# Where the last batch is cut: 24 of its 32 feed-forward steps over all 512 tokens, eight over halves, with the down projection of those eight summed on token partitions

## The chip, the core and the metric

The kernel runs on one core of a Trainium2 chip. The metric is the device time of one execution in microseconds (us). Matrix products run on the tensor engine (PE; its weight loads are shown as a row of their own, PEld), element-wise work on VectorE (DVE), ScalarE (ACT) and GpSimd (POOL). SyncE (SP) issues most of the transfers between on-chip memory and DRAM.

## What is computed

Eight batches of 512 tokens with 128 channels, all float32. For each batch, an attention part with linear cost, and then a dense sum over eight experts:

```python
x = x + layernorm(attention(layernorm(x)))
z = layernorm(x)
acc = 0
for wg, wu, wd in zip(Wg, Wu, Wd):          # 8 experts, 128 -> 512 -> 128
    acc += (silu(z @ wg) * (z @ wu)) @ wd
x = x + layernorm(acc)
```

The expert sum holds nearly all of the arithmetic: 8 experts times 4 slices of 128 hidden features are 32 steps for each batch.

## The kernel before

Channels (or hidden features) lie on the partitions and tokens along the free axis during a step. A step `i` takes one slice of 128 features: two products `g` (L928) and `u` (L930) with the weights `wg`, `wu` as the stationary operand and the normed tokens `zT` as the moving one; ACT makes `sg = silu(g)` (L932), and DVE makes `h = sg * u` (L939). The down projection then sums `wd.T @ h` over all 32 steps in PSUM. The order of instructions on each engine is the order in which the program issues them; no scheduler moves them. `g` and `u` have two PSUM buffers each, so the `u` product of step i+2 needs the `h` of step i to be done.

The work is cut into `units`. Batches 1 to 6 are one unit each, `WHOLE`, with 512 tokens. Batches 0 and 7 are two units each, `HALVES`, with 256 tokens and 32 steps.

- In a half unit, `down` (L768) is issued `LAG` = 2 steps after its `h`: one 128x256 product a step into `accA`, channels on the partitions.
- In a whole unit, the down projection goes over pairs of steps with seven block products in place of eight (Strassen's scheme). POOL makes the combinations `t` of `h` (L953 to L955), and `down_pairs` (L783, matmuls at L823) works off eight pairs at a time (`GROUP` = 16 steps), at step 17 of its unit and at step 1 of the next one, into the two banks `accA` and `accB`.
- `Last` finishes a whole batch during the next unit: `turn` (called at steps 2 and 3) transposes one bank in 32x32 blocks on DVE (`f_blkA`, `f_blkB`, L602) and `carry` (L261) sends it through DRAM by one write (L264) and four reads (L266) on SP's queue, which completes the transposition into `fA` and `fB`. Later `add` (seven DVE operations, L616 to L623) puts the seven products together into `q`, `stats`, `scales` and `norm` do the layer norm, and SP stores the result.
- The accumulator of a half unit has the same bank `accA`, of which there is one buffer.
- A half unit's sum is finished by a copy (L777), PE transposes (L258) and a norm in `finish`; the very last one by `finish_last` (L701): a copy by DVE and one by ACT (L717), two PE transposes (L721), bn_stats (L724), aggregation (L726), the power on POOL (L728), scaling, adding the residual and two stores (L737).

`plan(n)` names the step at which each of these pieces is issued, and `between(n)` runs them: at each step after `h` and before the down projections that have come due.

Of the kernel before, what the change touches and what calls it, by code (L numbers as in the profile page):

```python
# [16 lines left out]
def kernel(  # L17
# [10 lines left out]
    wd: bass.AP,  # L28
    out: bass.AP,
):  # L30

# [25 lines left out]
    nc = tc.nc  # L59
# [200 lines left out]

    def carry(dst, blocks):  # L261

        t = dram.tile([P, NQ, P], F32, tag="bounce", name="bounce")
        nc.sync.dma_start(t, blocks)  # L264
        for q in range(NQ):
            nc.sync.dma_start(  # L266
                dst[q * Q : (q + 1) * Q], t[:, q, :].rearrange("(r i) c -> i r c", r=NQ)
            )
# [21 lines left out]
        return t.rearrange("p j c -> p (j c)")  # L290

    def parts(b):
        return HALVES if b in (0, B - 1) else WHOLE

    x2s, zTs, rest = {}, {}, []

# [295 lines left out]
    class Last:  # L592
# [3 lines left out]
        def __init__(self, b, sums):  # L596
            self.b, self.sums, self.f = b, sums, []

        def turn(self):
            name = "AB"[len(self.f)]  # L600
            t = work.tile([P, NQ, P], F32, tag=f"blk{name}", name=f"f_blk{name}_{self.b}")
            nc.vector.transpose(  # L602
                t.rearrange("p a (s j k) -> p a s j k", s=2, j=2),
                self.sums[len(self.f)].rearrange("c (s a j i) -> c a s j i", s=2, a=NQ, j=2),
            )
            self.f.append(work.tile([P, NQ, P], F32, tag=f"f{name}", name=f"f{name}_{self.b}"))
            carry(self.f[-1], t)

        def add(self):
            A, D = (t.rearrange("p (t b) (s x) -> p t s b x", t=2, s=2) for t in self.f)  # L610
# [87 lines left out]
        nc.gpsimd.tensor_tensor(o, o, flat(x2s[b][:, r]), ALU.add)  # L698
        nc.sync.dma_start(out[b].rearrange("(p j) c -> p j c", j=NJ)[:, r], fn[:, :n])

    def finish_last(b, lo, hi, acc):  # L701


        n = hi - lo
        stats = small.tile([P, n, 6], F32, tag=f"stats{n}", name="stats_last")
        mv = small.tile([P, n, 2], F32, tag=f"mv{n}", name="mv_last")
        rstd = small.tile([P, n], F32, tag=f"rstd{n}", name="rstd_last")
        ve = small.tile([P, n], F32, tag=f"ve{n}", name="ve_last")
        fT = work.tile([P, N], F32, tag="fT", name="fT_last")
        fn = work.tile([P, NJ, C], F32, tag="fn", name="fn_last")  # L710
        o = work.tile([P, NJ, C], F32, tag="x1", name="o_last")
        acc = acc.rearrange("c (a j i) -> c a j i", a=NQ, j=n)
        dst = out[b].rearrange("(p j) c -> p j c", j=NJ)
        f_ps = []
        for j in range(n):
            cols = slice(j * P, (j + 1) * P)
            (nc.scalar.copy if j else nc.vector.tensor_copy)(  # L717
                fT[:, cols].rearrange("c (a i) -> c a i", a=NQ), acc[:, :, j]
            )
            t = ps.tile([P, N], F32, tag="ps", name=f"f_ps_last{j}")  # L720
            nc.tensor.transpose(t[:, :P], fT[:, cols], ident)  # L721
            f_ps.append(t)
        for j in range(n):
            nc.vector.bn_stats(stats[:, j, :], f_ps[j][:, :C])  # L724
        for j in range(n):
            nc.vector.bn_aggr(mv[:, j, :], stats[:, j, :])  # L726
        nc.vector.tensor_scalar_add(ve, mv[:, :, 1], EPS)
        nc.gpsimd.tensor_tensor(rstd, ve, mhalf[:, :n], ALU.pow)  # L728
        for j in range(n):
            nc.vector.tensor_scalar(  # L730
                fn[:, j, :], f_ps[j][:, :C], mv[:, j, 0:1], rstd[:, j : j + 1],
                ALU.subtract, ALU.mult,
            )
            (nc.vector if j else nc.gpsimd).tensor_tensor(
                o[:, j, :], fn[:, j, :], x2s[b][:, lo + j], ALU.add
            )
            (nc.scalar if j else nc.sync).dma_start(dst[:, lo + j], o[:, j, :])  # L737

    units = [(b, lo, hi) for b in range(B) for lo, hi in parts(b)]
    NSTEP = E * NF  # L740
    LAG = 2
    GROUP = 16
    HALF = C // 2
    accs, fins = {}, {}
    due = []
# [14 lines left out]
                    yield  # L760

    def down(n, i, h):
        b, lo, hi = units[n]
        if i == 0:
            accs[n] = ps_acc.tile([P, N], F32, tag="accA", name=f"acc_{n}")
        e, f = divmod(i, NF)
        cols = (hi - lo) * P
        nc.tensor.matmul(  # L768
            accs[n][:, :cols], wd_sb[e][:, f, :], h, start=(i == 0), stop=(i == NSTEP - 1)
        )  # L770
        if i == NSTEP - 1:
            acc = accs.pop(n)[:, :cols]
            if n == len(units) - 1:
                finish_last(b, lo, hi, acc)
                return
            fT = work.tile([P, N], F32, tag="fT", name=f"fT_{n}")
            nc.vector.tensor_copy(  # L777
                by_block(fT[:, :cols], hi - lo),
                acc.rearrange("c (a j i) -> c a j i", a=NQ, j=hi - lo),
            )  # L780
            fins[n] = finish(b, lo, hi, fT[:, :cols])

    def down_pairs(n, g, pairs):  # L783

        b, lo, hi = units[n]
        if g == 0:
            accs[n] = [  # L790
                ps_acc.tile([P, N], F32, tag=f"acc{t}", name=f"acc{t}_{n}") for t in "AB"
            ]
        A, D = accs[n]
        low, high = slice(0, HALF), slice(HALF, C)
        left, right = slice(0, N // 2), slice(N // 2, N)
        last = NSTEP // 2 - 1
        for two in range(0, len(pairs), 2):
            below, above = [], []
            for m, (h, t) in enumerate(pairs[two : two + 2]):
                k = g * GROUP // 2 + two + m  # L800
                e, pair = divmod(k, NF // 2)
                w0, w1 = wd_sb[e][:, 2 * pair], wd_sb[e][:, 2 * pair + 1]
                sm = ws_sb[e][:, pair]


                first, end = k == 0, k == last
                below += [
                    (A[low, left], w0[:, low], h[:, 0], first, False),
                    (A[low, right], w1[:, low], h[:, 2], False, end),
                    (D[low, right], sm[:, 3], h[:, 3], first, end),  # L810
                ]
                above += [
                    (D[high, right], sm[:, 0], t[:, 0], first, False),
                    (A[high, right], sm[:, 1], t[:, 2], first, False),
                    (D[high, left], sm[:, 2], t[:, 1], False, end),
                ]
                if m == 0:
                    below.append((D[low, left], w1[:, high], t[:, 3], False, False))
                else:
                    above.append((A[high, left], w1[:, high], t[:, 3], False, end))  # L820
            for two_tiles in zip(below, above):
                for o, w, r, start, stop in two_tiles:
                    nc.tensor.matmul(o, w, r, start=start, stop=stop)  # L823
        if (g + 1) * GROUP == NSTEP:
            fins[n] = Last(b, accs.pop(n))

    attentions = {}
# [5 lines left out]
    def plan(n):  # L833

        b, lo, hi = units[n]
        p = {i: [] for i in range(NSTEP)}

        def at(i, *calls):  # L840
            p[i] += calls

        following = attentions[b + 1] if 0 < b < B - 1 else None
        second = opened(b + 2) if hi == NJ and b + 2 < B else None
# [21 lines left out]
        if hi < NJ or lo:  # L866
            if second:
# [2 lines left out]
                at(23, second.norm)  # L870
                at(24, second.turn)
                at(31, second.affine)
            if last:
                at(14, last("add"))
                at(16, last("stats"))
                at(18, last("scales"))
                at(21, last("norm"))
        else:
            if second:
                at(17, second.stats, second.scales)  # L880
# [10 lines left out]

    def between(n):

        b, lo, hi = units[n]
        if lo == 0 and b + 2 < B:
            xs[b + 2] = load_x(b + 2)
        going = rest[:]
# [4 lines left out]
        if n == 1:  # L902
            going.append(attention(1))
        p = plan(n)
        for i in range(NSTEP):
            if isinstance(fins.get(n - 1), type(weight_sums())):
                going.append(fins.pop(n - 1))
            going = [g for g in going if next(g, "end") != "end"]
            for call in p[i]:
                call()  # L910
            yield
# [1 line left out]

    opening()
    count = 0
    for n, (b, lo, hi) in enumerate(units):
        zT = zTs.pop((b, lo))
        whole = hi - lo == NJ
        cols = (hi - lo) * P
        if whole:  # L920
            zT = zT.rearrange("c a (h j) i -> c h a (j i)", h=2)
            pairs = []
        others = between(n)
        for i in range(NSTEP):
            e, f = divmod(i, NF)
            w = bass.ts(f, P)
            g_ps = ps_gu.tile([P, N], F32, tag="g", name=f"g_{n}_{i}")
# [8 lines left out]
                h = flat(h2[:, 2 * (i % 2) : 2 * (i % 2) + 2])  # L936
            else:
                h = hp.tile([P, N // 2], F32, tag="h", name=f"h_{n}_{i}")
            nc.vector.tensor_tensor(h, sg[:, :cols], u_ps[:, :cols], ALU.mult)  # L939
            if not whole:  # L940
                due.append((count + LAG, partial(down, n, i, h)))
            elif i % 2:
                t2 = pairp.tile([P, 4, N // 2], F32, tag="t2", name=f"t2_{n}_{i}")
                pairs.append((h2, t2))
                if len(pairs) == GROUP // 2:
                    due.append((count + LAG, partial(down_pairs, n, i // GROUP, pairs)))
                    pairs = []
            next(others)
# [7 lines left out]
            count += 1  # L956
        for _ in others:
            pass
    for _, call in due:
        call()  # L960


# [29 lines left out]
```

## Time and profile before

| | |
|---|---|
| median of 3 runs | 708.70 us (708.69 to 709.01) |
| the profiled execution | 709.01 us |
| its span in the profile | 707.1 us |
| mean granted PE clock | 0.995 |
| PE busy | 692.7 us, 98% |
| POOL busy | 352.7 us, 50% |
| DVE busy | 299.0 us, 42% |
| ACT busy | 247.8 us, 35% |

A share is busy time over the span. Matmuls are pipelined, and the profile models their ends, so the busy time of PE overstates how full it is; for its pace the distance between the starts of successive matmuls is read. A float32 product of 128x128 by 128xN shows as two weight loads and two matmul records. The rows of a timeline give the start, the duration, the engine, the line, the operation, output and inputs, their sizes, how many instructions were merged, and in brackets how long the engine had been idle and what released it. The chain of waits merges neighbours in time, so its rows give a start and a length.

The last batch begins at 603.65 us, where its first `g` starts, and the span ends at 707.1 us.

### The profile page before, as it was taken

What the parts mean: (1) busy time and instruction counts of PE and PEld (TensorE: products, weight loads), DVE (VectorE), ACT (ScalarE), POOL (GpSimd) and SP (SyncE); (2) the same over time, 40 slices, a digit from 0 to 9 for tenths busy, and PEclk for the clock granted to TensorE, in tenths of its full rate; (3) what the DMA queues carried; (4) which work ended last, traced back from release to release, by engine and by line L of the source; (5) the groups of instructions that cost most, each with busy time, mean ns of one, the idle gap of its engine ahead of it and who ended that gap; (6) DMA issues with size and microseconds to landing.
All of it is one profiled execution on the core that took longest, in us unless ns stands there. A gap on an engine that the chain in (4) does not pass through costs nothing.

```text
span 707.1 us, 9148 instructions
## 1 busy us (share of the span) xinstructions
PE 692.7 (98%) x3149; PEld 420.2 (59%) x3149; DVE 299.0 (42%) x832; ACT 247.8 (35%) x497; POOL 352.7 (50%) x445
## 2 busy tenths in 40 slices
PE   8998999999999999999999999999999999999996
PEld 5787886454454545545455554555445454688885
DVE  5534463553425533354415634256332534134433
ACT  3322435334424334243333434334351423123231
POOL 3721121875647767385745867377673757301000
PEclk9999999999999999999999999999999999999998
DMA  8400001002011200102001020111101010010000
GB/s 265 156 1 0 8 0 58 25 1 75 0 53 37 71 21 29 60 1 90 0 31 59 17 75 0 45 45 47 31 15 64 12 46 1 1 59 17 8 0 8
DMA packets 31774, 27.14 MB, mean 38 GB/s; under 512 B 3440, under 2 KB 24176, under 8 KB 31728
## 3 DMA queue, kind: packets, MB, share of 16 engines
q1 hardware_dynamic: 31440, 26.36, 11.5%
q8 instruction: 25, 0.41, 0.3%
q14 instruction: 21, 0.17, 0.1%
q10 hardware_dynamic: 288, 0.20, 0.1%
HBM read 16.58 MB, written 9.96 MB: 38 GB/s over the span
## 4 chain that ended last, share of the span: by engine, by line
PE 93%; DVE 2%; issue 2%; POOL 1%; ACT 1%; DMA 0%; DVEq 0%; POOLq 0%
PE g L928 31%; PE u L930 30%; PE accA L823 12%; PE accB L823 9%; PE acc L768 7%; PE y_ps L559 1%; PE g_ps L476 1%; PE k_ps L534 1%; POOL rstd L186 0%; DMA x<-in_L_attn_x_dram 0%; DVE stats L180 0%; PE z_ps L258 0%; POOL x L450 0%; DVE stats L196 0%; POOL rstd L208 0%
## 5 line engine op out<-in xcount | busy, mean ns | idle before, releaser
L939 DVE TENSOR_TENSOR h<-sg,u 128x512 f32<-128x512 f32 (+1 forms) x320 | 185.5, 581 | 373.5 <-PE u L930 356.9
L932 ACT ACTIVATE sg<-g 128x512 f32<-128x512 f32 (+1 forms) x320 | 163.4, 512 | 397.9 <-PE g L928 375.1
L928 PE MATMUL g<-zT,wg 128*128 128x512 f32 (+1 forms) x640 | 274.4, 510 | 0.9 <-DVE zT L684 0.7
L930 PE MATMUL u<-zT,wu 128*128 128x512 f32 (+1 forms) x640 | 272.9, 508 | 0.2 <-DVE h L939 0.2
L930 PEld LDWEIGHTS u<-zT,wu 128*128 128x128 f32 x640 | 121.5, 190 | 99.7 <-issue 89.7
L953 POOL TENSOR_TENSOR t<-h 128x512 f32<-128x512 f32 x96 | 121.9, 1270 | 117.6 <-DVE h L939 117.6
L928 PEld LDWEIGHTS g<-zT,wg 128*128 128x128 f32 x640 | 118.1, 191 | 83.6 <-issue 74.9
L823 PE MATMUL accB<-t,ws 128*64 128x256 f32 x384 | 107.0, 381 | 0.0
L823 PE MATMUL accA<-h,wd 128*64 128x256 f32 x384 | 99.2, 381 | 0.0
L768 PE MATMUL acc<-h,wd 128*128 128x256 f32 x256 | 76.4, 381 | 1.3 <-DVE f_blkA L602 1.3
L954 POOL TENSOR_TENSOR t<-h,t 128x256 f32<-128x256 f32 x96 | 69.7, 726 | 7.5
L955 POOL TENSOR_TENSOR t<-h,t 128x256 f32<-128x256 f32 x96 | 69.6, 725 | 7.5
L823 PEld LDWEIGHTS accA<-h,wd 128*64 128x64 f32 x384 | 51.6, 137 | 34.7 <-issue 4.9
L823 PE MATMUL accA<-t,ws 128*64 128x256 f32 x192 | 57.1, 379 | 0.0
L823 PE MATMUL accB<-h,ws 128*64 128x256 f32 x192 | 57.1, 379 | 0.0
L234 POOL TENSOR_TENSOR rstd<-ve,mhalf 128x4 f32<-128x4 f32 (+1 forms) x24 | 28.1, 1170 | 54.1 <-DVE nm L232 46.7
L768 PEld LDWEIGHTS acc<-h,wd 128*128 128x128 f32 x256 | 47.9, 191 | 9.0 <-issue 3.1
L823 PEld LDWEIGHTS accB<-t,ws 128*64 128x64 f32 x384 | 51.6, 137 | 0.0
L823 PEld LDWEIGHTS accB<-h,ws 128*64 128x64 f32 x192 | 26.3, 137 | 13.9
L823 PE MATMUL accB<-t,wd 128*64 128x256 f32 x96 | 28.6, 379 | 0.0
L823 PE MATMUL accA<-t,wd 128*64 128x256 f32 x96 | 28.6, 379 | 0.0
L823 PEld LDWEIGHTS accA<-t,ws 128*64 128x64 f32 x192 | 26.3, 137 | 0.0
(185 smaller groups left out, 407.1 us busy)
## 6 DMA issues: line engine op xcount, KB each, us to landing
wg<-in_L_ffn_Wg_dram SPq DMA_DIRECT2D x8, 256.0 KB, 6.0
wu<-in_L_ffn_Wu_dram SPq DMA_DIRECT2D x8, 256.0 KB, 5.9
wd<-in_L_ffn_Wd_dram SPq DMA_DIRECT2D x8, 256.0 KB, 6.1
x<-in_L_attn_x_dram SPq DMA_DIRECT2D x7, 256.0 KB, 3.0
bounce<-xh_blk SPq DMA_DIRECT2D x6, 256.0 KB, 2.1
xhT<-bounce SPq DMA_DIRECT2D x24, 64.0 KB, 2.0
bounce<-ek_blk SPq DMA_DIRECT2D x6, 256.0 KB, 2.0
ek<-bounce SPq DMA_DIRECT2D x24, 64.0 KB, 2.0
```

The source lines that it names most:

```text
L234: nc.gpsimd.tensor_tensor(rstd, ve, mhalf[:, :n], ALU.pow)
L476: nc.tensor.matmul(g_ps[:, :C], xh[:, j, :], ek[:, :, j * Q : (j + 1) * Q], start=(j == 0), stop=(j == NJ - 1),)
L534: nc.tensor.matmul(k_ps, w_qkv_sb[:, C : 2 * C], self.xnT, start=True, stop=True)
L768: nc.tensor.matmul(accs[n][:, :cols], wd_sb[e][:, f, :], h, start=(i == 0), stop=(i == NSTEP - 1))
L823: nc.tensor.matmul(o, w, r, start=start, stop=stop)
L928: nc.tensor.matmul(g_ps[:, :cols], wg_sb[e][:, w], zT, start=True, stop=True)
L930: nc.tensor.matmul(u_ps[:, :cols], wu_sb[e][:, w], zT, start=True, stop=True)
L932: nc.scalar.activation(sg[:, :cols], g_ps[:, :cols], AF.Silu)
L939: nc.vector.tensor_tensor(h, sg[:, :cols], u_ps[:, :cols], ALU.mult)
L953: nc.gpsimd.tensor_tensor(t2[:, 0:2], h2[:, 1::2], h2[:, 0:2], ALU.subtract)
L954: nc.gpsimd.tensor_tensor(t2[:, 2], h2[:, 3], t2[:, 0], ALU.subtract)
L955: nc.gpsimd.tensor_tensor(t2[:, 3], h2[:, 2], t2[:, 2], ALU.subtract)
```

## The change

Batch 7 becomes three units: all 512 tokens for steps 0 to 23, then tokens 0 and 1 of each group of four (256 tokens) for steps 24 to 31, then the other 256 tokens for steps 24 to 31. The first 24 steps use the paired scheme, so this batch has a group of eight pairs at step 17 and one of four pairs at step 25, which is in the first half unit. For the last eight steps a class `End` takes the place of `down` and `finish_last`: `h` is the stationary operand and `wd` the moving one, so the sum has tokens on the partitions. DVE writes `h` with its columns in another order for that.

The part of the sum that the first 24 steps made goes the way of `Last`: `turn_both` transposes both banks at step 26 of the first half unit, issuing the two writes ahead of the eight reads; `add` runs at step 26 of the second half unit, eight half steps later. Its result `q` is added to each half's PSUM sum by a product with the identity (`earlier`). The first half is normed and stored at steps 28 and 29 of the second half unit; the last one in `finish`, without the copy and the transposes. The downs of the last two steps are issued with the first 128 tokens ahead of the second.

```diff
     def parts(b):
-        return HALVES if b in (0, B - 1) else WHOLE
+        return HALVES if b == 0 else WHOLE
...
+        def turn_both(self):
+            out = [carry_out(self.blocks()) for _ in range(2)]
+            for f, t in zip(self.f, out):
+                carry_in(f, t)
...
+    class End:
...
+        def __init__(self, b, lo, hi):
+            self.b, self.lo, self.n = b, lo, hi - lo
+            self.acc = ps.tile([P, N], F32, tag="ps", name=f"acc_{b}_{lo}")
+            self.f = self.acc[:, : self.n * C].rearrange("p (j c) -> p j c", c=C)
+            self.begun = False
+
+        def down(self, i, h, j, end=False):
+            e, f = divmod(i, NF)
+            self.add(h[:, j * P : (j + 1) * P], wd_sb[e][:, f, :], j, end)
+
+        def add(self, w, moving, j, end):
+            nc.tensor.matmul(self.f[:, j, :], w, moving, start=not self.begun, stop=end)
+            self.begun = True
+
+        def earlier(self, src, end):
+            for j in range(self.n):
+                self.add(ident, src[self.lo + j], j, end and j == self.n - 1)
...
+        def finish(self):
...
+            for j in range(n):
+                nc.vector.bn_stats(stats[:, j, :], self.f[:, j, :])
+            for j in range(n):
+                nc.vector.bn_aggr(mv[:, j, :], stats[:, j, :])
...
-    units = [(b, lo, hi) for b in range(B) for lo, hi in parts(b)]
+    SPLIT = 24
+    units = [(b, lo, hi, 0, NSTEP) for b in range(B - 1) for lo, hi in parts(b)]
+    units.append((B - 1, 0, NJ, 0, SPLIT))
+    units += [(B - 1, lo, hi, SPLIT, NSTEP) for lo, hi in HALVES]
...
+        if begin:
+            whole = next(m for m in range(n) if units[m][0] == b)
+            if not lo:
+                at(26, lambda: fins[whole].turn_both())
+            else:
+                at(26, lambda: fins[whole].add())
+                at(28, lambda: ends[0].earlier(fins[whole].src, True), lambda: ends[0].norm())
+                at(29, lambda: ends[0].store(), lambda: ends[lo].earlier(fins[whole].src, False))
+            return p
...
-            nc.vector.tensor_tensor(h, sg[:, :cols], u_ps[:, :cols], ALU.mult)
-            if not whole:
+            if begin:
+                nc.vector.tensor_tensor(
+                    by_block(h, hi - lo),
+                    *(t[:, :cols].rearrange("c (a j i) -> c a j i", a=NQ, i=Q) for t in (sg, u_ps)),
+                    ALU.mult,
+                )
+            else:
+                nc.vector.tensor_tensor(h, sg[:, :cols], u_ps[:, :cols], ALU.mult)
+            if begin:
+                call = partial(ends[lo].down, i, h)
+                if lo and i >= NSTEP - LAG:
+                    left.append(call)
+                else:
+                    due.append((count + LAG, lambda call=call: [call(j) for j in range(2)]))
...
-                if len(pairs) == GROUP // 2:
+                if len(pairs) == GROUP // 2 or i == end - 1:
...
-    for _, call in due:
-        call()
+    for j in range(2):
+        for call in left:
+            call(j, end=call is left[-1] and j == 1)
+    ends[lo].finish()
```

## The prediction

> **What bounds the kernel now.** I read the page first, then the chain of waits, then the timeline of the last batch. On the page PE is busy 98% of the span, and the chain that ended last is 93% PE:
>
> ```profile
> PE 692.7 (98%) x3149; PEld 420.2 (59%) x3149; DVE 299.0 (42%) x832; ACT 247.8 (35%) x497; POOL 352.7 (50%) x445
> ...
> PE 93%; DVE 2%; issue 2%; POOL 1%; ACT 1%; DMA 0%; DVEq 0%; POOLq 0%
> ```
>
> So a gain must be PE time, a PE stall, or something after the last matmul. The pace of a half step of the last batch, from the timeline:
>
> ```profile
> 689.50 0.59 PE L928 MATMUL g<-zT,wg 128*128 128x256 f32 x2
> ...
> 690.36 0.59 PE L768 MATMUL acc<-h,wd 128*128 128x256 f32 x2
> 690.79 0.59 PE L928 MATMUL g<-zT,wg 128*128 128x256 f32 x2
> ```
>
> From `g` to `g` is 1.295 us (20 steps from 622.37 take 25.90): three slots of 0.432, with no gap. A whole step is quicker per token: six `g`/`u` slots of 512 from 582.19 to 592.49 give 0.858 each, 1.717 a step. The paired down projection, from the chain:
>
> ```profile
> 606.55 0.86 PE accB L823 x8
> 609.58 0.86 PE accB L823 x8
> ```
>
> 3.02 us for two pairs, so 1.512 a pair. Going in and out of a group costs more: in the timeline of batch 6,
>
> ```profile
> 566.32 1.02 PE L930 MATMUL u<-zT,wu 128*128 128x512 f32 x2
> ...
> 580.47 1.02 PE L930 MATMUL u<-zT,wu 128*128 128x512 f32 x2
> ```
>
> 14.15 us, less one step of 1.717, leave 12.43 for eight pairs: 12.09 and 0.34 for the two borders.
>
> The last batch has one stall. Its first `down` must wait until DVE has emptied `accA`:
>
> ```profile
> 618.24 0.59 PE L930 MATMUL u<-zT,wu 128*128 128x256 f32 x2
> ...
> 620.14 0.67 PE L768 MATMUL acc<-h,wd 128*128 128x256 f32 x2 [1.30 <-DVE f_blkA L602]
> 620.64 0.59 PE L928 MATMUL g<-zT,wg 128*128 128x256 f32 x2
> ```
>
> By starts, 620.64 is 1.54 us later than two slots after 618.24. All of it adds up: 64 half steps 82.88, batch 6's second group 12.43, the stall 1.54, two transposes in mid-batch 0.22 make 97.07; from 603.65 to the end of the last slot at 700.73 is 97.08.
>
> Then the tail:
>
> ```profile
> 699.43 1.46 PE L768 MATMUL acc<-h,wd 128*128 128x256 f32 x6
> 699.70 0.42 DVE L939 TENSOR_TENSOR h<-sg,u 128x256 f32<-128x256 f32 x1 [0.87 <-PE u L930]
> 700.92 0.29 DVE L717 COPY fT_last<-acc 128x128 f32<-128x128 f32 x1 [0.81 <-PE acc L768]
> ...
> 701.64 0.59 DVE L724 BATCH_NORM_STATS2 stats_last<-f_ps_last 128x6 f32<-128x128 f32 x2 [0.42 <-PE f_ps_last L721]
> ```
>
> **The change, part by part.**
>
> *The first 24 steps.* 48 half steps go: 48 x 1.295 = 62.16. In their place come 24 x 1.717 = 41.20, twelve pairs 18.14, and two groups' borders 0.68: 60.02. **-2.14.** POOL gets 12 pairs of 1.27 + 0.73 + 0.73, about 2.9 us with its gaps, against 3.4 us in which two steps arrive, as in batches 1 to 6. At step 25 the last pair's `t` is needed: `h` of step 23 is done 1 us after its `u`, POOL some 2.9 later. PE gets there after two half steps (1.73), but the last pair's first `t` is the 22nd of 28 products, 4.5 us on. Without that cover it would be a stall of 2.2.
>
> *The stall.* `accA` of batch 7 is now first written at step 17, long after `f_blkA` at step 2: **-1.54.** Next late would be `u` of step 4, which needs `h` of step 2; the transposition of 0.71 stands behind that `h`, and behind `h` of step 3 comes `f_blkB`, as in batches 2 to 6, where PE shows no stall.
>
> *The last 16 half steps.* `g` and `u` keep their slots. `down` turns from two passes of 256 columns under one pair of loads into four passes of 128 under four loads of `h`. The nearest row is `y_ps`, four products of 128 columns with four different stationaries, eight passes:
>
> ```profile
> 550.84 1.05 PE L559 MATMUL y_ps<-wa,xnT 128*128 128x128 f32 x8
> 551.73 1.02 PE L928 MATMUL g<-zT,wg 128*128 128x512 f32 x2
> ...
> 550.84 0.86 PEld L559 LDWEIGHTS y_ps<-wa,xnT 128*128 128x128 f32 x7 [0.24 <-issue]
> ```
>
> 0.89 for eight, 0.445 for four: 0.013 over the old slot, **+0.21** for 16. [...] The row has full-array loads, each 190 ns long, at one per 111 ns under the matmuls, [...]; I take 111.
>
> The new write order of `h` is that of L777, 0.42 us for 128x256, no more than L939's 0.42. By that row it costs nothing, being hidden in DVE's 0.87 of idle time a step; were it twice as long, it would still fit.
>
> *turn_both.* Two transpositions of 0.71 at step 26 hold up `h` of step 27. `h` ends 1.12 after its `u` starts, and 1.42 more makes 2.54, where `h` of 27 would start by itself at 2.0: 0.54 late. `u` of step 29 leaves 1.5 (two steps of 1.31 less 1.12). Nothing. On SP two writes and eight reads are issued; only batch 6's store is ahead of them, and behind them the first half's. Before, the way of one bank was
>
> ```profile
> 620.02 0.34 SPq L264 DMA_DIRECT2D bounce<-f_blkA  x1
> 622.04 1.74 SPq L266 DMA_DIRECT2D fA<-bounce  x4
> 623.88 0.38 SPq L264 DMA_DIRECT2D bounce<-f_blkB  x1
> 625.96 1.73 SPq L266 DMA_DIRECT2D fB<-bounce  x4
> ```
>
> 2.0 to land, 1.74 to issue the reads, 2.0 more. With both writes ahead, the eighth read lands some 7.7 us after `f_blkA`. `add` comes eight half steps, 10.5, less 0.7, later: 2 us to spare. What waits behind `add` on DVE is the `h` of step 27 and through it PE.
>
> *add and earlier.* The seven DVE operations ended 2.10 us after the start of the `h` ahead of them (636.02 to 638.12). Here that `h` starts 0.70 after `u` of 26, so `q` is there at 2.80; PE asks for it at the end of `u` of 28, at 3.05. Taken as no stall, with 0.25 of cover: a wait of 0 to 0.6. The four identity products are 8 passes of the `y_ps` kind, **+0.89**; the two old mid-batch transposes go, **-0.22**. Norm and store of the first half lie in DVE's and POOL's idle time, as `finish` did.
>
> *The tail.* `h` of step 31 ends 1.12 after its `u` starts. Before, its `down` was third and came at 1.29. Now the second of the last products needs it at 1.10, and as a stationary: 0.06 for the semaphore and as much before the pass. A new wait, with all that is left queued behind it: **+0.15** (0 to 0.35; no row has just this). Copy and transposes go: bn_stats starts where the copy did, 700.92 in place of 701.64, **-0.72**. In the changed kernel's instruction order the first bn_stats waits and the second does not, so both stand behind the last matmul; the order of tokens gains nothing.
>
> **Sum:** -2.14 - 1.54 + 0.21 + 0.89 - 0.22 + 0.15 - 0.72 = -3.37. The profiled execution took 709.01 (1.9 around its span of 707.1), so 705.64; it was the slowest of the three runs, 0.31 over the median. From the median: 708.70 - 3.37 = **705.3**.
>
> **The rivals.**
> *Loads of `h` are not hidden (slower).* Place: the `down` of the 16 half steps. [...] It decides from 53 ns a load (3.37/64). Against it, `y_ps`; for it, that `y_ps` is one burst between long slots, where here four loads come each 1.3 us. 5%.
> *The way through DRAM is late.* [...] Each us over the 2 to spare stops DVE, then PE after 0.2: two to three us late give 706 to 708. Landings are 1.8 to 2.7 throughout, so 6%.
> *Small waits add up* (`add` before `earlier`, the wait for the last `h`, borders of the short group): 705.8 to 706.7. 14%.
> *Change without effect:* the paired scheme earns only 2.14; if the lost stall came back at step 4 and the tail's wait were 0.7, some 707.4, within what counts as same. 3%.
>
> **How the numbers follow.** Forecast 72%, 704.6 to 705.8; the rivals have the rest. The range, 704.4 to 706.8, takes in the small waits and the lower part of the DRAM case. About 0.2%, 1.4 us, is what a measurement of this kernel can tell from no change. Faster 0.91 (forecast, small waits, most of the DRAM case), same 0.04, slower 0.05.
>
> **What would show it.** Right: 128x128 `acc` passes 111 ns apart; no idle PE at the first step 2; `g` to `g` 1.31 in the half steps; bn_stats about 0.03 after the last matmul. Wrong: PE idle for DVE in the last unit's steps 28 to 29, DVE idle for a DMA at `add`, or half steps of over 1.4.

## The result, and the profile after

The changed kernel takes 705.45 us (median of 6 runs, 704.27 to 706.04), the kernel before 708.84 (6 runs with the three above among them, 707.54 to 709.18): the medians are 3.4 us apart. The ratio is 0.9957, with a 95% interval of 0.9946 to 0.9969, which is 2.2 to 3.8 us less. Runs of either kernel differ by some 1.6 us, most likely over something that happens in batch 0, which the change doesn't touch (last section), so what a part is worth is read below from the stage that begins with the first `g` of batch 7, and not from the run times alone.

The profiled execution took 705.33 us, with a span of 703.5 and a mean granted clock of 0.997. On its page, the busy time of each engine, and the shares of the chain that ended last:

```profile
PE 690.5 (98%) x3161; PEld 397.5 (56%) x3161; DVE 297.5 (42%) x815; ACT 243.8 (35%) x472; POOL 386.1 (55%) x481
...
PE 94%; issue 2%; DVE 2%; POOL 1%; ACT 1%; DVEq 0%; POOLq 0%
```

PE still sets the time. POOL has 33 us more work, the `t` of twelve more pairs, and no `t` stands in the chain. In the PE timeline of after, the beginning of batch 7, its step 2, and two of the half steps:

```profile
603.33 1.02 PE L976 MATMUL g<-zT,wg 128*128 128x512 f32 x2
...
619.09 1.12 PE L976 MATMUL g<-zT,wg 128*128 128x512 f32 x2
620.05 1.02 PE L978 MATMUL u<-zT,wu 128*128 128x512 f32 x2
620.91 1.02 PE L976 MATMUL g<-zT,wg 128*128 128x512 f32 x2
...
694.13 0.60 PE L976 MATMUL g<-zT,wg 128*128 128x256 f32 x2
694.56 0.59 PE L978 MATMUL u<-zT,wu 128*128 128x256 f32 x2
694.99 0.61 PE L733 MATMUL acc<-wd,h 128*128 128x128 f32 x4
695.44 0.60 PE L976 MATMUL g<-zT,wg 128*128 128x256 f32 x2
```

At step 2, where `accA` made PE wait before, each slot now follows the last by 0.86 to 0.96. A half step is 1.31 from `g` to `g`: two slots of 0.43, and 0.45 for the four passes that take `h` as the stationary operand. Then the end, in the timeline of after:

```profile
696.30 1.68 PE L733 MATMUL acc<-wd,h 128*128 128x128 f32 x12
696.57 0.42 DVE L988 TENSOR_TENSOR h<-sg,u 128x256 f32<-128x256 f32 x1 [0.89 <-PE u L978]
698.02 0.50 DVE L764 BATCH_NORM_STATS2 stats_last<-acc 128x6 f32<-128x128 f32 x2 [1.03 <-PE acc L733]
698.43 0.30 DVE L766 BATCH_NORM_AGGREGATE mv_last<-stats_last 128x2 f32<-128x6 f32 x2
...
700.73 0.36 SPq L777 DMA_DIRECT2D out_dram<-o_last  x1
```

In the timeline of before, the last store on SP:

```profile
704.44 0.33 SPq L737 DMA_DIRECT2D out_dram<-o_last  x1
```

Set beside the trace of before (us):

| | before | after | difference |
|---|---|---|---|
| first `g` of batch 7 | 603.65 | 603.33 | -0.32 |
| from there to the first read of the last sum (copy, now bn_stats) | 97.27 | 94.69 | -2.58 |
| from there to bn_stats | 97.99 | 94.69 | -3.30 |
| from there to the issue of the last store on SP | 100.79 | 97.40 | -3.39 |

The first row is unchanged code, and differs between executions. The last row is the change: -3.39, where the sum said -3.37. The experiments take it apart.

### The profile page after: what moved, and what is told of

Read it like the earlier page. It is cut to its first block, busy times and chain, and to the rows that moved or that the text cites. A ratio compares the mean times of both kernels' runs of the same rounds, so it can differ in the third digit from the quotient of the medians.

```text
span 703.5 us, 9130 instructions
## 1 busy us (share of the span) xinstructions
PE 690.5 (98%) x3161; PEld 397.5 (56%) x3161; DVE 297.5 (42%) x815; ACT 243.8 (35%) x472; POOL 386.1 (55%) x481
## 4 chain that ended last, share of the span: by engine, by line
PE 94%; issue 2%; DVE 2%; POOL 1%; ACT 1%; DVEq 0%; POOLq 0%
PE g L976 31%; PE u L978 30%; PE accA L863 13%; PE accB L863 10%; PE acc L811 3%; PE acc L733 1%; PE y_ps L566 1%; PE g_ps L483 1%; PE k_ps L541 1%; PE unread L165 1%; POOL rstd L187 0%; DVE stats L181 0%; PE z_ps L259 0%; POOL x L457 0%; POOL rstd L209 0%
## 5 line engine op out<-in xcount | busy, mean ns | idle before, releaser
L994 DVE TENSOR_TENSOR h<-sg,u 128x512 f32<-128x512 f32 (+1 forms) x280 | 175.1, 626 | 356.2 <-PE u L978 340.9
L1014 POOL TENSOR_TENSOR t<-h 128x512 f32<-128x512 f32 x108 | 137.4, 1272 | 140.6 <-DVE h L994 140.6
L978 PEld LDWEIGHTS u<-zT,wu 128*128 128x128 f32 x592 | 112.4, 190 | 108.7 <-issue 100.9
L976 PEld LDWEIGHTS g<-zT,wg 128*128 128x128 f32 x592 | 107.9, 191 | 91.7 <-issue 86.2
L863 PE MATMUL accB<-t,ws 128*64 128x256 f32 x432 | 120.4, 381 | 0.0
L863 PE MATMUL accA<-h,wd 128*64 128x256 f32 x432 | 111.6, 381 | 0.0
L1016 POOL TENSOR_TENSOR t<-h,t 128x256 f32<-128x256 f32 x108 | 78.6, 727 | 8.5
L1015 POOL TENSOR_TENSOR t<-h,t 128x256 f32<-128x256 f32 x108 | 78.5, 727 | 8.5
L863 PE MATMUL accA<-t,ws 128*64 128x256 f32 x216 | 64.2, 379 | 0.0
L863 PE MATMUL accB<-h,ws 128*64 128x256 f32 x216 | 64.2, 379 | 0.0
L811 PE MATMUL acc<-h,wd 128*128 128x256 f32 x128 | 38.6, 383 | 0.0
```

The source lines that it names most:

```text
L811: nc.tensor.matmul(accs[n][:, :cols], wd_sb[e][:, f, :], h, start=(i == 0), stop=(i == NSTEP - 1))
L976: nc.tensor.matmul(g_ps[:, :cols], wg_sb[e][:, w], zT, start=True, stop=True)
L978: nc.tensor.matmul(u_ps[:, :cols], wu_sb[e][:, w], zT, start=True, stop=True)
L1014: nc.gpsimd.tensor_tensor(t2[:, 0:2], h2[:, 1::2], h2[:, 0:2], ALU.subtract)
L1015: nc.gpsimd.tensor_tensor(t2[:, 2], h2[:, 3], t2[:, 0], ALU.subtract)
L1016: nc.gpsimd.tensor_tensor(t2[:, 3], h2[:, 2], t2[:, 2], ALU.subtract)
```

## The experiments

Every ratio is to the kernel before, run on the same chip. "Stage" is the time from the first `g` of batch 7 to the first read of the last sum by DVE, or to what is named.

**The stall alone.** Before, with the sums of batch 7's two units in the pool of short-lived banks, so that they need not wait for `accA`:

```diff
-            accs[n] = ps_acc.tile([P, N], F32, tag="accA", name=f"acc_{n}")
+            pool, tag = (ps, "ps") if b == B - 1 else (ps_acc, "accA")
+            accs[n] = pool.tile([P, N], F32, tag=tag, name=f"acc_{n}")
```

> The kernel before, with one thing changed: the sums of the last batch's two halves take a bank of the pool ps in place of accA, so the first down of that batch waits for nobody. From the batch's first g to the last copy (97.27 us before). My sum: the stall of 1.54 goes and nothing comes in its place, 95.7 us, and the time is 1.5 under the kernel before. Rival (the stall only moves, to a u product that needs an h standing behind the transposition f_blkA on DVE): 97 us, the same time as before.

It took 706.02 us (5 runs), ratio 0.9969 (0.9956 to 0.9981). The first and the last row of the stage, from its timeline:

```profile
604.04 0.59 PE L929 MATMUL g<-zT,wg 128*128 128x256 f32 x2
...
699.77 0.29 DVE L717 COPY fT_last<-acc 128x128 f32<-128x128 f32 x1 [0.80 <-PE acc L769]
```

95.73 instead of 97.27: the stall was worth 1.54, all of it, and no wait took its place. So nearly half of what the change gains needs neither the split nor the other way of summing, only another bank. (The medians are 3.0 apart: three of the five runs are near 706.0 and two near 707.7, and the last section says what probably sets such groups apart.)

**Tokens on the partitions alone.** Both halves of batch 7 keep all their 32 steps, and all of these sum with tokens on the partitions:

```diff
-        return HALVES if b == 0 else WHOLE
+        return HALVES if b in (0, B - 1) else WHOLE
...
-    units.append((B - 1, 0, NJ, 0, SPLIT))
-    units += [(B - 1, lo, hi, SPLIT, NSTEP) for lo, hi in HALVES]
+    units += [(B - 1, lo, hi, 0, NSTEP) for lo, hi in HALVES]
...
+        if b == B - 1 and lo:
+            at(2, lambda: ends[0].norm())
+            at(3, lambda: ends[0].store())
             return p
...
-        zT = zTs[b, 0][:, :, lo:hi] if begin else zTs[b, lo]
+        zT = zTs[b, lo]
+        tokens = b == B - 1
...
-        if begin:
+        if tokens:
             ends[lo] = End(b, lo, hi)
```

> Only the second part of the change: the last batch stays two halves of 32 steps each, without pairs, but all of its down projections have h as the stationary operand and tokens on the partitions; no transposes at the end, nothing added through the identity. My sum: 64 half steps of 1.308 in place of 1.295 (+0.83), no stall (-1.54), no transposes in mid-batch (-0.22), the wait for the last h (+0.2): first g to bn_stats 96.5 us, then -0.72 for the tail: 1.5 under the kernel before. Rival (this part carries the whole gain, the pairs none): 3.4 under it. [...]

This first form left out the add, the norm and the store of batch 6. It took 707.52 us, ratio 0.9977 (0.9968 to 0.9987), stage 96.66. The second form has batch 6's end again:

```diff
+            if last:
+                at(14, last("add"))
+                at(16, last("stats"))
+                at(18, last("scales"))
+                at(21, last("norm"))
```

> The kernel of e2_tokens, which left out the last norm and the store of batch 6, with these put back at the steps where the kernel before has them: two halves of 32 steps, no pairs, tokens on the partitions in the down projection. Nothing of what was left out runs on PE, so the same as e2_tokens: half steps of 1.308, first g to bn_stats 96.66 us, and 1.5 under the kernel before. Rival (batch 6's work on DVE and ACT costs PE something beside the new down projection): more than 97 us.

It took 706.21 us (6 runs), ratio 0.9975 (0.9961 to 0.9989). From its timeline, the beginning of the stage, the `g` of two successive steps in its middle, and the end:

```profile
602.24 0.59 PE L976 MATMUL g<-zT,wg 128*128 128x256 f32 x2
...
660.94 0.60 PE L976 MATMUL g<-zT,wg 128*128 128x256 f32 x2
...
662.25 0.60 PE L976 MATMUL g<-zT,wg 128*128 128x256 f32 x2
...
698.89 0.49 DVE L764 BATCH_NORM_STATS2 stats_last<-acc 128x6 f32<-128x128 f32 x2 [1.03 <-PE acc L733]
```

The half step is again 1.31, now over 64 of them and with nothing else on PE, so the four loads of `h` cost no more over all 64 than in after, where a load is 0.19 long and the next one starts 0.11 after it. The stage is 96.65, 0.62 less than before. It adds up: the stall goes here too, since the sums have other banks (-1.54), 64 half steps are longer by 0.015 (1.31 instead of 1.295, +0.96), two transposes go (-0.22), and the last `h` is waited for as in after (+0.19): -0.61. With the 0.72 at the end this form gains some 1.3 in all. The other 2.0 of the change (96.65 less 94.69) come from the pairs, after what adding their sum costs.

**Four more or four fewer paired steps.** The cut after 20 steps instead of 24:

```diff
-    SPLIT = 24
+    SPLIT = 20
...
-                at(26, lambda: fins[whole].turn_both())
+                at(22, lambda: fins[whole].turn_both())
```

> The changed kernel with the cut at step 20 in place of 24 (turn_both at step 22). My sum: four steps with two pairs (4 x 1.717 + 2 x 1.512 = 9.89) are replaced by eight half steps of 1.308 (10.46), so 0.57 over the changed kernel, 2.8 under the one before; the borders cost the same. First g to bn_stats 94.69 -> 95.26 us. Rival (the pairs earn nothing on this chip, the gain is the stall and the tail): no difference from the changed kernel or less time.

704.86 us (5 runs), ratio 0.9948 (0.9936 to 0.9961). The run times can't tell this from after, but the stage can, 603.40 to 698.69 in its timeline:

```profile
603.40 1.02 PE L976 MATMUL g<-zT,wg 128*128 128x512 f32 x2
...
698.69 0.49 DVE L764 BATCH_NORM_STATS2 stats_last<-acc 128x6 f32<-128x128 f32 x2 [1.03 <-PE acc L733]
```

95.29 against 94.69: four steps, moved from two pairs to eight half steps, cost 0.60. Worked out by the prediction's prices (eight half steps of 1.308, less four steps of 1.717 and two pairs of 1.512) it is 0.57, and with the half step of 1.31 that was measured, 0.59. So by an estimate from these two cuts each further pair would earn 0.3, as long as the way through DRAM keeps its cover. The other way, with 28 steps and the earlier sum added after everything else:

```diff
-    SPLIT = 24
+    SPLIT = 28
...
-                at(26, lambda: fins[whole].turn_both())
+                at(30, lambda: fins[whole].turn_both())
...
-                at(26, lambda: fins[whole].add())
-                at(28, lambda: ends[0].earlier(fins[whole].src, True), lambda: ends[0].norm())
-                at(29, lambda: ends[0].store(), lambda: ends[lo].earlier(fins[whole].src, False))
+                at(31, lambda: fins[whole].add())
...
+    src = next(f for f in fins.values() if isinstance(f, Last) and f.b == B - 1).src
+    ends[lo].earlier(src, True)
     ends[lo].finish()
+    ends[0].earlier(src, True)
+    ends[0].norm()
+    ends[0].store()
```

> The changed kernel with the cut at step 28: turn_both at step 30 of the first half, add at step 31 of the second, five half steps later in place of eight, and the identity products after the last downs, the second half first. My sum: the steps gain 0.57, but the way through DRAM takes 7.7 us from f_blkA against 5.8 until add, and add (2.1), the identity products and two norms now follow one another with nothing beside them. DVE waits 2 us for fA, the last bn_stats stands 5 to 6 us behind the changed kernel's, the time is 3 to 5.5 over it, about that of the kernel before or worse. Rival (the transfer is quick enough when nothing else moves): no wait at add, 1 to 2.5 over the changed kernel.

709.84 us (20 runs, 708.48 to 711.96), ratio 1.0019 (1.0011 to 1.0027): more than all of the gain is gone. Its timeline shows the wait go from the DMA to DVE and from DVE to PE:

```profile
695.84 0.29 DVE L634 TENSOR_TENSOR fB<-fB,fA 128x128 f32<-128x128 f32 x1 [1.12 <-DMA fB<-bounce]
...
697.25 1.16 PE L733 MATMUL acc<-q,ident 128*128 128x128 f32 x8 [1.95 <-DVE q L639]
...
700.75 0.48 DVE L181 BATCH_NORM_STATS2 stats<-acc 128x6 f32<-128x128 f32 x2
...
704.03 0.36 SPq L749 DMA_DIRECT2D out_dram<-fn  x1
```

DVE waits 1.12 for `fB` (the expectation put 2 on `fA`, which was there in time), PE 1.95 for `q`, and the norm of one half follows the norm of the other, so the first half's is the last. From the first `g` (602.13 here) the last store is issued after 101.90, against 97.40. This is what the rival of the late transfer looks like where it is real; with 24 steps it isn't.

**The order of the transfers.** `turn_both` issues both writes ahead of the reads. One bank after the other:

```diff
-            out = [carry_out(self.blocks()) for _ in range(2)]
-            for f, t in zip(self.f, out):
-                carry_in(f, t)
+            for _ in range(2):
+                self.turn()
```

> The changed kernel with turn_both undone: the two banks go through DRAM one after the other, so the second write stands behind the first one's four reads on SP. My sum: the last read of fB lands 9.9 us after f_blkA in place of 7.7; add starts 9.8 after it and touches fB 0.4 later, so no wait or 0.2, and the time of the changed kernel within 0.3. Rival (the way through DRAM has no slack): DVE waits 2 us at add, PE after it, and the time is 1.5 to 2 over the changed kernel.

705.6 us (4 runs), ratio 0.9947 (0.9932 to 0.9963), stage 603.79 to 698.49, which is 94.70: no difference. In its timeline the second write stands behind the first four reads, and `add` still runs without a wait:

```profile
684.06 0.38 SPq L268 DMA_DIRECT2D bounce<-f_blkB  x1
...
686.14 1.73 SPq L273 DMA_DIRECT2D fB<-bounce  x4
...
690.34 0.28 DVE L633 TENSOR_TENSOR fB<-fB,fA 128x128 f32<-128x128 f32 x1
```

In after, from the same view, both writes are out before the reads:

```profile
680.32 0.32 SPq L268 DMA_DIRECT2D bounce<-f_blkB  x1
681.79 1.75 SPq L273 DMA_DIRECT2D fA<-bounce  x4
683.63 1.80 SPq L273 DMA_DIRECT2D fB<-bounce  x4
```

The issue of the reads ends at 685.43, and `add` starts at 689.47 in after. With 2 us to land, as before (the median of the reads of `fB` is 2.0 in after too), that leaves about 2 us, the estimate of the prediction. One bank after the other, the issue ends at 687.87; counted from the first `g` of each trace that is 2.0 later (84.08 against 82.10). The last read then lands at about 689.9, and the first operation of `add` that takes `fB` starts at 690.34: it just fits.

**The tail.** The last half gets a bank for each of its two blocks of 128 tokens (`accA` and `accB`, free by then), and its last products are issued step by step, so that the first block's bn_stats need not stand behind all of them:

```diff
...
-            nc.tensor.matmul(self.f[:, j, :], w, moving, start=not self.begun, stop=end)
-            self.begun = True
+            bank = j if self.lo else 0
+            nc.tensor.matmul(self.banks[j], w, moving, start=bank not in self.begun, stop=end)
+            self.begun.add(bank)
...
-    for j in range(2):
-        for call in left:
-            call(j, end=call is left[-1] and j == 1)
+    for call in left:
+        for j in range(2):
+            call(j, end=call is left[-1])
```

> The changed kernel with another tail: the last half sums its two token blocks in two banks (accA and accB, free by then), and the last four products go step by step, so the two that need h of step 31 come last. My sum: PE does not wait for that h (the gap of 0.19 between weight loads goes), and the first bn_stats no longer stands behind the last matmul. From the first g to the aggregation 95.10 -> 94.7 us, the time 0.4 under the changed kernel. Rival (the 0.19 is something else, a cost of these products that moves with them): the gap stays between the loads, 0.2 at most is won.

705.54 us (5 runs), ratio 0.9949 (0.9937 to 0.9961). From its timeline:

```profile
697.69 0.30 PEld L740 LDWEIGHTS accA<-wd,h 128*128 128x128 f32 x2
697.92 0.30 PEld L740 LDWEIGHTS accB<-wd,h 128*128 128x128 f32 x2
698.03 0.39 PE L740 MATMUL accB<-wd,h 128*128 128x128 f32 x2
698.23 0.30 DVE L771 BATCH_NORM_STATS2 stats_last<-accA 128x6 f32<-128x128 f32 x1 [0.62 <-PE accA L740]
698.45 0.30 DVE L771 BATCH_NORM_STATS2 stats_last<-accB 128x6 f32<-128x128 f32 x1
698.67 0.30 DVE L773 BATCH_NORM_AGGREGATE mv_last<-stats_last 128x2 f32<-128x6 f32 x2
```

Its first `g` is at 603.94, so the aggregation comes after 94.73; in after it is 698.43 - 603.33 = 95.10. That is 0.37 less, hidden in run times that scatter by four times as much. Two things make it up. The last weight loads now follow each other without the gap of 0.19 that after has at the last `h` (0.23 for two); and the first bn_stats starts 0.19 before the last product ends (698.42), where both bn_stats of after stood behind it (697.98 and 698.02). How much of the second is due to the banks and how much to the order of the products was not taken apart.

**The identity products.** On top of the last kernel, the first half's two identity products (four passes) become two additions on DVE; the last half keeps its own:

```diff
-                at(28, lambda: ends[0].earlier(fins[whole].src, True), lambda: ends[0].norm())
+                at(28, lambda: ends[0].plus(fins[whole].src), lambda: ends[0].norm())
...
+        def plus(self, src):
+            t = work.tile([P, NJ, C], F32, tag="y", name="sum_first")
+            for j in range(self.n):
+                d, a = (v.rearrange("p (b k) -> p b k", b=NQ) for v in (t[:, j], self.f[:, j]))
+                nc.vector.tensor_tensor(d, a, src[self.lo + j], ALU.add)
+            self.f = t[:, : self.n]
```

> As e5_tail, and the first half adds its earlier sum on DVE (two operations of 128x128, some 0.33 each) in place of two products with the identity. My sum: PE saves 0.445, DVE has room for 0.7 at step 28; first g to the aggregation 94.25 us, the time 0.45 under e5_tail and 0.85 under the changed kernel. Rival (DVE becomes the bound in steps 28 to 30: h of 29 and 30 come late, PE waits): as e5_tail or slower.

703.36 us (6 runs, 703.34 to 705.16), ratio 0.9934 (0.9921 to 0.9946). From its timeline:

```profile
690.94 0.48 DVE L751 TENSOR_TENSOR sum_first<-acc,q 128x128 f32<-128x128 f32 x2
...
696.46 0.30 DVE L780 BATCH_NORM_AGGREGATE mv_last<-stats_last 128x2 f32<-128x6 f32 x2
```

With the first `g` at 602.18 that is 94.28, 0.45 less than 94.73: PE saves the 0.44 of four passes, and the 0.48 on DVE costs nothing, since PE shows no wait for an `h` there.

**The gap in batch 0.** Two runs on what moves the run times. The first is the kernel before, with batch 1's attention begun four steps later and with one step put between the first norm's statistics and what needs them; nothing of batch 7 is changed:

```diff
+    def later(steps):
+        for _ in range(4):
+            yield
+        next(steps)
+        yield
+        yield
+        yield from steps
...
-            going.append(attention(1))
+            going.append(later(attention(1)))
```

> The kernel before with another place for the start of batch 1's attention: its first piece is issued four steps later in batch 0's second half and one step is left between its statistics and xh. In the kernel before, DVE waits there for POOL's power (1.65 us), the copy L777 stands behind it, and PE is idle for 2.67 us at 66 to 69 us; in most profiles the granted clock is then 0.5 for 3.4 us, in some not. My sum: the idle 2.67 goes, and the dip with it, which is worth about 1.4: 2.7 to 4.1 under the kernel before, no run slower than the others by 1.4, mean clock 1.00. Rival (the dip comes by itself, whatever PE does): 2.7 under it, the clock still 0.5 for 3.4 us in most runs and the times still in two groups. Rival (the attention pieces press later and the stall moves): no gain.

705.39 us (5 runs, 705.35 to 705.47), ratio 0.9957 (0.9943 to 0.9971). By the medians as much as the whole change, from a few lines elsewhere; against the faster runs of before, at about 707.5, it is 2.1. The second puts the same edit on the last kernel of the series:

> e7_tail_dve with the later start of batch 1's attention. The last batch is as in e7_tail_dve, first g to the aggregation 94.28 us; the stall of 2.67 and the dip in batch 0 go as in e9_late_before. By my sum 700.7 us, 8 under the kernel before and 4.7 under the changed one; if the dip stays, 702.

701.25 us (4 runs, 701.19 to 701.39), ratio 0.9898 (0.9885 to 0.9912): 7.5 us less than before and 4.2 less than after, the best version here. From its timeline:

```profile
600.11 0.59 PE L998 MATMUL g<-zT,wg 128*128 128x512 f32 x1
...
694.39 0.30 DVE L788 BATCH_NORM_AGGREGATE mv_last<-stats_last 128x2 f32<-128x6 f32 x2
```

Its stage to the aggregation is 94.28 again, the same to a hundredth in two kernels with the same last batch. The two gains add up: counted from the faster runs of before, 2.11 for the late attention and 4.15 for the last kernel (its faster runs are at 703.35) make 6.26, and 701.25 is 6.25 below. The medians, 7.5 apart, hold the loss of the slower group as well.

## Why the prediction was right

*The first 24 steps, -2.14.* Measured the same. From the first `g` to the `g` of the first half step are 66.07 us (603.33 to 669.40): the prediction's 41.20, and 24.87 for two groups of 12.43. One of these is batch 6's second group, so the four pairs of the short group are still to come; in the PE timeline, the third and fourth `g` of the first half unit:

```profile
677.41 0.70 PE L976 MATMUL g<-zT,wg 128*128 128x256 f32 x2
...
678.82 0.60 PE L976 MATMUL g<-zT,wg 128*128 128x256 f32 x2
```

From 669.40 to 677.41 are four slots of 0.432, four pairs (6.05) and 0.24; the next step is 1.41, 0.10 longer than those after it. Together 0.34, the border that the prediction took from batch 6. PE had no idle time there: POOL had its products `t` ready.

*The stall, -1.54.* Measured alone: 1.54. The prediction's claim that no other wait stands behind it held in the trial and in after.

*The last 16 half steps, +0.21.* Measured +0.24: 1.31 each, the prediction's 1.308 and some. The row of the trace that it chose, four different full-array stationaries in 0.445, was the right price: 111 ns for a load and its pass. In after the loads of `h` are 0.19 long and start 0.11 apart, like those of that row. The prediction's rival of loads that are not hidden needed 53 ns more a load to undo the gain (3.37/64), by that estimate 0.21 more a half step; the half steps of 1.31 in the kernel with all of batch 7 on token partitions leave no room for it.

*`add` and `earlier`, +0.89.* The timeline of after, at the place where PE takes the sum over:

```profile
690.80 0.42 DVE L639 TENSOR_TENSOR q<-q,fB 128x256 f32<-128x256 f32 x1
...
691.05 0.59 PE L978 MATMUL u<-zT,wu 128*128 128x256 f32 x2
...
691.48 0.61 PE L733 MATMUL acc<-q,ident 128*128 128x128 f32 x4
691.92 0.61 PE L733 MATMUL acc<-wd,h 128*128 128x128 f32 x4
...
692.37 0.60 PE L976 MATMUL g<-zT,wg 128*128 128x256 f32 x2
```

`q` is done at 691.22, PE takes it at 691.48: a cover of 0.26, where the prediction had 0.25. Each pair of identity products takes 0.45 (692.37 to 694.13 from `g` to `g` where the last half's stand, 1.76 instead of 1.31).

*The way through DRAM, no cost.* It held with some 2 us to spare, shown from the other side by the cut after 28 steps, where it was late.

*The tail, +0.15 - 0.72.* The wait for the last `h` shows in the weight loads of after, which otherwise follow each other in 0.11:

```profile
696.75 0.19 PEld L733 LDWEIGHTS acc<-wd,h 128*128 128x128 f32 x1
697.05 0.19 PEld L733 LDWEIGHTS acc<-wd,h 128*128 128x128 f32 x1
```

0.30 apart, so a wait of 0.19; `h` ends at 696.99 and is loaded 0.06 later. The copy and the transposes went as said. What was not foreseen is that the two bn_stats take 0.50 where they took 0.59, -0.09; why was not looked into.

By what was measured, the sum is -2.14 - 1.54 + 0.24 + 0.90 - 0.22 + 0.19 - 0.72 - 0.09 = -3.38, and the table has -3.39. So each term held to a tenth, and the small errors (+0.03, +0.01, +0.04, -0.09) nearly cancel. What the prediction did not see is that runs of one kernel differ by 1.6 us: it had three runs within 0.3, and gave its range no room for that. That this did no harm is luck: four of the six runs of after, and five of the six of before, lie in the slower group. With most runs of after in the faster one, as the kernel with the additions on DVE had it, the median would have been about 704.3, under the range, with every term of the sum as it is.

## What to carry to other kernels

Add up the stage slot by slot until the sum meets the trace to a hundredth, as the 97.07 did here: then a stall has nowhere to hide, and each part of a change can be priced from a row for the same kind of instruction. Before reorganizing a sum, ask whether the wait at its beginning is only one for a bank, since another bank was worth 1.5 of the 3.4 us here. Where run times come in two groups, find what the groups are made of before measuring effects smaller than their distance, and compare stages in the traces until then.

## What was not expected of the hardware

In batch 0 of before, from its timeline, PE stands idle for 2.67 us:

```profile
67.24 1.11 DVE L249 TENSOR_SCALAR xh<-x,mv,rstd 128x128 f32<-128x128 f32 x4 [1.43 <-POOL rstd L208]
...
68.74 0.69 PE L258 MATMUL f_ps<-ident,fT 128*128 128x128 f32 x2 [2.67 <-DVE fT L777]
```

DVE waits for POOL's power with `xh`, the copy that PE needs is queued behind `xh`, and PE waits for that copy. What then happens to the clock, from the view of stretches (length, busy time and count of each engine, the granted clock, the share of the DMA, GB/s), first before, then the kernel with the additions on DVE, then before with the late attention:

```profile
68.00:70.00 2.00, 1.26 (x4) 1.16 (x5) 1.54 (x8) 0.00 (x0) 0.00 (x0) 0.57 0.00 0
70.00:72.00 2.00, 2.00 (x8) 1.51 (x7) 0.35 (x3) 0.38 (x1) 0.70 (x1) 0.58 0.00 0
```

```profile
68.00:70.00 2.00, 1.32 (x7) 1.22 (x8) 1.76 (x9) 0.00 (x0) 0.00 (x0) 1.00 0.00 0
```

```profile
68.00:70.00 2.00, 2.00 (x11) 1.76 (x10) 1.85 (x8) 0.67 (x2) 0.88 (x2) 1.00 0.00 0
```

In the profiles of before, after and four of the experiments the clock falls to half at this gap (to 0.50), for 3.4 us where its end was read (before, after, the cut after 20 steps, the other tail); in those of four others it stays at 1.00, with the same gap of 2.67. Products slow down with it: in before, `u` starts 0.85 after `g` in the dip (70.08 and 70.93), and 0.43 ahead of the gap (65.04 and 65.48). By stretches of 0.2 us it falls at 68.3 in before, when PE has been idle for 2.2 us and is not yet back; it is the same in after (2.2) and in the cut after 20 steps (2.3). In the other three it falls 0.5 to 1.4 after PE is back. Half speed for 3.4 us is some 1.7 us lost, and less where a part of it falls into the gap: the first `g` of batch 7 starts at 602.1 to 602.2 without the dip, at 603.3 to 603.7 where it begins in the gap, and at 603.8 to 604.0 where it begins behind it.

That is about the distance of the two groups of run times: 707.2 to 707.7 and mostly 708.6 to 709.3 for before, 704.3 and 705.3 to 706.0 for after. Of the runs without a profile only the time and the mean granted clock are known, and the clock doesn't sort all of them (708.68 of before has the 0.998 of the faster group); that all slower runs had the dip is therefore likely, not shown. A gap of 2.67 us came with the dip in six of ten profiles. Where the gap is taken away neither profile shows the dip, and the runs of such a kernel lie within 0.2 us of each other. Against the faster runs of before the late attention still gains 2.1 and not 2.67; in its trace PE's waits for `h` and for `sg` from 60 to 110 us are 0.8 and 0.6, where before has 0.2 for `h`. What decides which run has the dip was not shown.
